# A feed-forward schedule that treats the last token of every 512 by itself

## The chip, the cores and the metric

One core of one Trainium2 chip runs the whole program. The metric is the device time of one execution in microseconds (us). Engines: PE (matmul), DVE (vector), ACT (scalar), POOL (GpSimd) and SP (which only issues DMAs here).

## The reference, cut to what matters

`x` holds 2048 tokens of 256 features, the context 1601. A cross-attention with four heads of 64 runs first, then a feed-forward with quantized weights and activations:

```python
x = x + xattn(ctx, layernorm(x), mask, ...)      # keys: 1601 of the context and the 2048 tokens
x = x + ffn(layernorm(x), w1, conv_w, conv_b, w2)

def ffn(x, w1, conv_w, conv_b, w2):
    h = bit_linear(x, w1)                        # 256 -> 1024, rows of x rounded to 8 bits each
    h = depthwise_conv1d(h, conv_w, conv_b)      # over the tokens, 3 taps: t-1, t, t+1
    return bit_linear(silu(h), w2)               # 1024 -> 256, rows rounded again
```

The convolution is all that couples neighbouring tokens in the feed-forward: a token needs the hidden values of the one before and the one behind it.

## The kernel before, in words

**Stages.** A prologue loads and normalizes the tokens and makes keys, values and queries. Then comes a loop of 80 beats. A unit is 512 queries of one pair of heads; there are 8 units (0 to 7), two for each 512 tokens, of ten beats each, and a beat takes three of the 29 blocks of 128 keys (the last beat of a unit two). In a beat PE makes the scores `st`, ACT their exponentials `pt`, and PE multiplies these with the values into `ot`. The sum of the exponentials is collected beside that: some `pt` are added into `acc` and `acd` by DMAs that POOL issues, the others into `vec` by DVE. In the second and third beat of the next unit DVE joins the sums, PE adds them up into `dn`, and DVE takes its reciprocal and divides (`finish_unit`, line 683).

After every second unit the 512 tokens that are complete go through `block_steps` (727) in four blocks of 128, one a beat from the sixth beat of the next unit on: output projection `po`, residual and statistics, normalization, rounding to 8 bits, and a transpose into `xq_all` (rounded features by token) with the factors of the tokens, repeated on all partitions, in `ib_all`.

**The feed-forward** works on eight groups of 256 tokens (0 to 7), each in four slots of 256 of the 1024 hidden values. A slot has `hidden` (809, four matmuls into `ph` for 258 tokens, one more at either end), `dequantize` (820, DVE: `h` = `ph` times `ib_all`), `taps` and `last_tap` (829, 846: the convolution into `pre` on ACT, DVE and POOL) and `silu` (856, ACT, into `t`; in the loop it needs another activation table than the exponential, and one is loaded before and behind it). After its slots a group has `magnitudes` (912: `m`, the largest value of each token, in two halves), `columns` and `scales` (920, 926: `m` transposed by PE into `tpa`, reduced by DVE to `am`, factors `qsc`, and on POOL `cm`), `scales_spread` (934: `cm` transposed into `tpb` and copied by ACT to `tb`), `rounding` (940: two halves of the hidden values, each a product into `t` and a rounding into `hq`), and `product` (950: for each 128 tokens eight matmuls `py`, then on DVE `res` = `py` times factor plus residual, and on SP the store).

**The order** is written out by hand. `plan` holds calls by beat (`at`, 594), and `feed_forward(g, k, slots)` (964) enters those of a group whose first slot is at beat k: `hidden` and `dequantize` at k-1, then a slot every second beat; `columns` and `scales` at k+11, `scales_spread` and the first `rounding` at k+13, the second at k+14, `product` at k+15. Group 1 ends at token 511, whose convolution needs token 512, which is complete some 20 beats later than token 511. Before, groups 0 to 3 begin at beats 30, 48, 56 and 68, and the first slot of group 4 at beat 76 (1000). Each engine carries out its instructions in the order of the program (`InOrder`, 162).

**Behind the loop** (from line 1060 on) two of the three taps of half a slot move to PE, as matmuls with diagonal matrices (`end_taps`, `end_convolve`, `end_last_tap`, `end_silu`). The last 512 tokens go through the block steps (`head`, 1100), and beside them `tick(i)` (1119) takes one slot after another, 15 slots in all: three of group 4 and those of groups 5, 6 and 7. What `plan` still holds (the end of group 3) is called one call per tick (`rest`, 1115). Each `product` makes its `res` at once. `compare` of the last unit follows at tick 15, and the flag `behind` is made at the very end; by it the program decides whether a second, slower version of the layer has to run (it does not here).

**PSUM.** In the loop three double banks (`big`, 153) hold `st`, `ph` and `py` in turn, one bank holds `ot`, and a single bank (`bank`, 156, one buffer) serves `dn`, `tpm`, `tpa`, `tpb`, `po` and `tpy` in turn.

Of the kernel before, what the change touches and what calls it, by code (L numbers as in the profile page):

```python
# [10 lines left out]
F32 = mybir.dt.float32  # L11
# [8 lines left out]
P = 128  # L20
# [9 lines left out]
def layer(  # L30
# [86 lines left out]
    OFF = 1  # L117
    xq_all = const.tile([P, ND, NL + 2 * OFF], BF16, name="xq_all")
    units1 = const.tile([P, NQB], F32, name="units1")
    for edge in (OFF - 1, OFF + NL):  # L120
        nc.gpsimd.memset(xq_all[:, :, edge : edge + 1], 0.0)

    q_un = [const.tile([P, NPAIR * QW], F32, name=f"q_un{g}") for g in range(NU)]
# [29 lines left out]
    def big(name):  # L153
        return ps_b.tile([P, 2, 512], F32, tag="big", name=name)
# [442 lines left out]

    def quant_scales(amax, n, vector=nc.vector):

        vector.tensor_scalar(amax, amax, QUANT_EPS, None, ALU.max)  # L600
        sc = sm.tile([P, QPG], F32, tag="qsc", name="qsc")
        vector.reciprocal(sc[:, :n], amax)
        vector.tensor_scalar(sc[:, :n], sc[:, :n], 127.0, None, ALU.mult)
        return sc

    def product_units(amax, i):

        vector.tensor_scalar(amax, amax, w_mean[:, i : i + 1], 1.0 / 127.0, ALU.mult, ALU.mult)

    def as_rows(cols, n):  # L610

        cm = sm.tile([P, QPG, P], F32, tag="cm", name="cm", bufs=3)
        for i in range(n):
            gpsimd.tensor_scalar(cm[:, i, :], ones, cols[:, i : i + 1], None, ALU.mult)
        return cm

    def repeat_rows(tp, cm):

        for i in range(QPG):
            tensor.transpose(tp[:, i, :], cm[:, i, :], ident)  # L620
# [6 lines left out]
    with att:  # L627
# [166 lines left out]

        fp = att.enter_context(tc.tile_pool(name="fp", bufs=1 if behind is None else 2))
        ib_all = fp.tile([P, NL + 2], F32, name="ib_all", bufs=1)
        for edge in (0, NL + 1):
            nc.gpsimd.memset(ib_all[:, edge : edge + 1], 0.0)

        NP = NH // 2  # L800
# [1 line left out]
        groups_ = [{} for _ in range(NG)]  # L802
        chunk = {}
        where = {
            "ph": big, "py": lambda: big("py")[:, 0, :D],
            "t": lambda: fp.tile([P, G, NC2], F32, tag="t", name="t", bufs=3),
        }

# [11 lines left out]
        def dequantize(s):  # L820
            t0 = s // NP * G
            h = fp.tile([P, 2, G + 2], F32, tag="h", name="h", bufs=2)
            vector.tensor_tensor(
                h, chunk[s]["ph"][:, :, : G + 2],
                ib_all[:, t0 : t0 + G + 2].unsqueeze(1).to_broadcast([P, 2, G + 2]), ALU.mult,
            )
            chunk[s]["h"] = h
# [74 lines left out]
        def end_silu(s, j):  # L902
            g, c = s // NP, s % NP * 2
            if c % NC2 == 0 and j == 0:
                groups_[g].setdefault("t", []).append(where["t"]())
            t = groups_[g]["t"][c // NC2][:, :, c % NC2 + j]
            if j == 0:
                scalar.activation(t, chunk[s]["ph"][:, 0, :G], AF.Silu, bias=cb_sb[:, c : c + 1])
            else:
                scalar.activation(t, chunk.pop(s)["pre"][:, 1, :], AF.Silu)  # L910
# [12 lines left out]
            for i in range(QPG):  # L923
                tensor.transpose(b["tp"][:, i, :], b["m"][:, ts(i, P)], ident)

        def scales(g):
            b = groups_[g]
            b["unit"] = sm.tile([P, QPG], F32, tag="am2", name="am2")
            vector.tensor_reduce(b["unit"], b.pop("tp"), AX.X, ALU.max)
            sc = quant_scales(b["unit"], QPG, vector)  # L930
            b["cm"] = as_rows(sc, QPG)
            product_units(b["unit"], 1)

        def scales_spread(g):
            tb = bank("tpb", [P, QPG, P])
            repeat_rows(tb, groups_[g].pop("cm"))
            groups_[g]["tb"] = fp.tile([P, G], F32, tag="tb", name="tb")
            scalar.copy(groups_[g]["tb"], tb.rearrange("p i t -> p (i t)"))

        def rounding(g, i):  # L940
            b = groups_[g]
            t = b["t"][i]
            vector.tensor_tensor(
                t, t, b["tb"].unsqueeze(2).to_broadcast([P, G, NC2]), ALU.mult
            )
            if i == 0:
                b["hq"] = fp.tile([P, G, NH], BF16, tag="hq", name="hq", bufs=1)
            vector.tensor_scalar(b["hq"][:, :, ts(i, NC2)], t, MAGIC, -MAGIC, ALU.add, ALU.add)

        def product(g, i):  # L950
            b = groups_[g]
            py = where["py"]()
            for c in range(NH):
                tensor.matmul(
                    py, b["hq"][:, ts(i, P), c], w2T[:, c, :], start=(c == 0), stop=(c == NH - 1)
                )
            qb = g * QPG + i
            res = fp.tile([P, D], F32, tag="res", name="res")
            vector.scalar_tensor_tensor(
                res, py, b["unit"][:, i : i + 1], x1[qb], ALU.mult, ALU.add  # L960
            )
            nc.sync.dma_start(out_t[:, qb, :], res)

        def feed_forward(g, k, slots, pace=2):

            for n in range(slots):
                s, t = g * NP + n, k + n * pace
                for m, call in (
                    (-1, hidden), (-1, dequantize), (0, taps), (1, last_tap), (3, silu),
                ):  # L970
                    at(t + m, lambda call=call, s=s: call(s), LATE)
                if n % 2:
                    at(t + 4, lambda n=n: magnitudes(g, n // 2), LATE)
            if slots < NP:
                return
            t = k + NP * pace
            for m, call in (
                (3, columns), (3, scales), (5, scales_spread), (5, lambda g: rounding(g, 0)),
                (6, lambda g: rounding(g, 1)), (7, lambda g: product(g, 0)),
                (7, lambda g: product(g, 1)),  # L980
            ):
                at(t + m, lambda call=call: call(g), LATE)

# [12 lines left out]
        for j in beats[0]:  # L996
            pts[0, j] = exponential(0, j, early.pop(0) if early else scores(0, j))

        for g, k in enumerate((30, 48, 56, 68)):
            feed_forward(g, k, NP)  # L1000
        feed_forward(4, 76, 1)
        at(NB * len(units) - 6, lambda: diagonals(0), LATE)
        at(NB * len(units) - 2, lambda: diagonals(1), LATE)

# [60 lines left out]
        def y_bank(name):  # L1065
            return ps_y.tile([P, QW], F32, tag="y", name=name)

        where.update(
            ph=lambda name: ps_h.tile([P, 2, 512], F32, tag="ph", name=name),
            py=lambda: y_bank("py")[:, :D],  # L1070
            t=lambda: ptp.tile([P, 2, QW], F32, tag="pt", name="t").rearrange(
                "p h q -> p (h q)"
            ).rearrange("p (t c) -> p t c", c=NC2),
# [38 lines left out]
                if i < NSUB:  # L1112
                    run(i, RESIDUAL, INVERSE)

        rest = [call for key in sorted(plan) for call in plan.pop(key)]
        slots = list(range(4 * NP + 1, NG * NP))
        N = len(slots)

        def tick(i):
            if 0 <= i - 2 < N:  # L1120
                end_silu(slots[i - 2], 1)
            if 0 <= i - 1 < N:
                end_silu(slots[i - 1], 0)
            if i < N:
                dequantize(slots[i])
            if 0 <= i - 1 < N:
                end_last_tap(slots[i - 1])
            if i < N:
                end_taps(slots[i])
            for g in range(4, NG):  # L1130
                n = i - ((g - 4) * NP - 1)
                if n == 4:
                    magnitudes(g, 0)
                if n == 6:
                    magnitudes(g, 1)
                    columns(g)
                    scales(g)
                if n == 7:
                    scales_spread(g)
                if n == 8:  # L1140
                    rounding(g, 0)
                    rounding(g, 1)
            if i + 1 < N:
                hidden(slots[i + 1])
            if i < N:
                end_convolve(slots[i])
            if 1 <= i <= NSUB:
                run(i - 1, TURN)
            for g in range(4, NG):
                if i == (g - 4) * NP + 7:  # L1150
                    product(g, 0)
                    product(g, 1)

        for sub in range(NSUB):
            run(sub, BIAS)
        hidden(slots[0])
        for i in range(N + 6):
            head(i)
            tick(i)
            if i >= 2 and rest:  # L1160
                rest.pop(0)()
            if i == N:
                compare(len(units) - 1, r)
        assert not rest

    if behind is not None:
        worst = sm.tile([P, 1], F32, tag="worst", name="worst")
        nc.vector.tensor_reduce(worst, near, AX.X, ALU.min)
        nc.vector.tensor_scalar(worst, worst, 0.5, None, ALU.is_lt)
        many = bank("many", [P, 1])  # L1170
        nc.tensor.matmul(many, ones, worst, start=True, stop=True)
        nc.vector.tensor_copy(behind, many)


@with_exitstack
# [41 lines left out]
```

## Time and profile before

| | before |
|---|---|
| median of 3 runs | 695.08 us (694.35 to 696.06) |
| the profiled execution | 695.91 us, span of its instructions 693.9 us |
| mean granted PE clock | 0.973 |
| busy: PE, DVE, ACT, POOL | 630.2, 465.6, 423.5, 277.3 us |
| loop, first to last `ot` matmul | 113.0 to 590.9 us |
| behind the loop | 590.9 to 693.9 us |
| activation table loads | 34, 1283 ns each |

The page cuts the span in 40 slices of 17.3 us and gives each engine's busy share in tenths. All matmul and vector calls are recorded at one line of a helper (L170), so instructions are told apart by their tiles: `py<-w2T,hq` is the matmul that writes `py` from `w2T` and `hq`. A row of the timeline has start, length, engine, operation, tiles and shapes, and in brackets the idle time of the engine before it and what ended that.

### The profile page before, as it was taken

To read this page: it belongs to the slowest core of one execution; us is meant where nothing else is said; L and a number is where in the kernel's file an instruction comes from. 1 tells how busy PE (TensorE), PEld (TensorE's weight loads), DVE (VectorE), ACT (ScalarE), POOL (GpSimd) and SP (SyncE) were. 2 spreads that over 40 slices of the span, in tenths; PEclk is the share of its full clock that TensorE was granted. 3 is DMA by queue.
4 is the path that set the end of the run, shared out by engine and by line. 5 is a ranking of instruction groups with operands and counts; after the bars stand their busy time and mean duration, and the time that the engine had idled before them with its cause. 6 is when DMAs were issued, how large, how long until landed. Compare 5 with 4: busy or idle time off the path is not lost. (4 is left out here: it accounts for less than half of the span.)

```text
span 693.9 us, 8026 instructions
## 1 busy us (share of the span) xinstructions
PE 630.2 (91%) x2796; PEld 266.8 (38%) x2796; DVE 465.6 (67%) x790; ACT 423.5 (61%) x534; POOL 277.3 (40%) x333
## 2 busy tenths in 40 slices
PE   4999898999999999999999999998899999766753
PEld 2555563333333333333334333333333433445532
DVE  3658774332822865696387779667976889895884
ACT  2556556555555544679845478997576799254440
POOL 2656663211221335244154444434344466432220
PEclk9999999999999999999999999999999999988985
DMA  7600003684876765478658447865474555000000
GB/s 238 169 0 1 0 1 102 128 161 96 182 144 160 151 122 106 113 132 166 152 128 161 92 106 140 167 133 141 93 147 91 142 100 109 0 0 17 15 31 20
DMA packets 32220, 72.12 MB, mean 104 GB/s; under 512 B 7531, under 2 KB 16940, under 8 KB 32172
## 3 DMA queue, kind: packets, MB, share of 16 engines
q0 software_dynamic: 16560, 60.30, 42.9%
q1 hardware_dynamic: 14524, 10.45, 5.1%
q10 hardware_dynamic: 1088, 0.79, 0.3%
q8 instruction: 24, 0.39, 0.2%
q14 instruction: 24, 0.20, 0.1%
HBM read 9.13 MB, written 2.10 MB: 16 GB/s over the span
## 5 line engine op out<-in xcount | busy, mean ns | idle before, releaser
L170 ACT ACTIVATE pt<-st,bias 128x1024 f32<-128x1024 f32 x232 | 242.9, 1113 | 123.9 <-issue 63.0
L170 PE MATMUL st<-q_un,kT 64*128 64x512 f32 x928 | 222.2, 607 | 5.0 <-DVE res L170 1.8
L170 PE MATMUL ot<-pt,v_sb 128*64 128x512 f32 x928 | 216.6, 600 | 0.1
L170 DVE TENSOR_TENSOR vec<-vec,pt 128x1024 f32<-128x1024 f32 x107 | 137.5, 1285 | 40.3 <-ACT pt L170 36.3
L170 PEld LDWEIGHTS st<-q_un,kT 64*128 64x128 f32 x928 | 82.7, 186 | 124.6 <-issue 89.3
L170 PEld LDWEIGHTS ot<-pt,v_sb 128*64 128x64 f32 x928 | 60.2, 136 | 136.9 <-issue 130.4
L170 POOL DMA_DIRECT2D acd<-pt x54 | 44.9, 832 | 127.2 <-ACT pt L170 60.7
L170 POOL DMA_DIRECT2D acc<-pt x61 | 52.7, 864 | 69.6 <-ACT pt L170 51.2
L170 POOL TENSOR_TENSOR pre<-pre,side 128x512 f32<-128x512 f32 (+1 forms) x32 | 38.4, 1201 | 57.0 <-DVE pre L170 51.8
L170 PE MATMUL kv<-wkv_sb,feat 128*128 128x512 f32 (+1 forms) x116 | 53.6, 605 | 0.0
L170 ACT ACT_TABLE_LOAD x34 | 43.6, 1283 | 16.2 <-DMA lb<-in_L_xattn_ln_l_b_dram 7.5
L170 POOL TENSOR_TENSOR ss<-ss,neg_half 128x8 f32<-128x8 f32 (+1 forms) x23 | 39.2, 1702 | 1.9
L170 POOL TENSOR_SCALAR cm<-ones,units 128x128 f32<-128x128 f32 x16 | 11.8, 739 | 60.1 <-DVE units L170 57.7
L170 DVE TENSOR_TENSOR h<-ph,ib_all 128x516 f32<-128x516 f32 x32 | 22.0, 687 | 20.1 <-PE ph L170 18.5
L170 DVE TENSOR_REDUCE ss<-sq 128x8 f32<-128x512 f32 (+1 forms) x23 | 15.5, 672 | 29.7 <-ACT sq L170 29.5
L170 DVE COPY oT<-ot 128x512 f32<-128x512 f32 x8 | 5.5, 692 | 44.0 <-PE ot L170 43.9
L170 PE MATMUL ph<-h,dg 128*128 128x256 f32 x90 | 25.9, 430 | 7.3 <-DVE h L170 7.3
L170 ACT ACTIVATE t<-pre 128x512 f32<-128x512 f32 (+1 forms) x32 | 29.7, 929 | 2.3 <-POOL pre L170 2.0
L170 DVE RECIPROCAL r<-dn 128x512 f32<-128x512 f32 (+1 forms) x11 | 27.3, 2480 | 5.6 <-PE dn L170 5.6
L170 PEld LDWEIGHTS kv<-wkv_sb,feat 128*128 128x128 f32 (+1 forms) x116 | 21.4, 193 | 22.4 <-issue 21.5
L170 ACT ACTIVATE side<-h,cw_sb 128x256 f32<-128x256 f32 x66 | 29.7, 507 | 0.0
L170 PE MATMUL py<-w2T,hq 128*128 128x256 bf16 x128 | 20.5, 318 | 8.3 <-DVE hq L170 8.3
(128 smaller groups left out, 712.2 us busy)
## 6 DMA issues: line engine op xcount, KB each, us to landing
acc<-pt POOLq DMA_DIRECT2D x61, 512.0 KB, 5.1
acd<-pt POOLq DMA_DIRECT2D x54, 512.0 KB, 4.7
tok<-in_x_dram SPq DMA_DIRECT2D x4, 512.0 KB, 6.0
w_sb<-in_L_ffn_w_dram SPq DMA_DIRECT2D x4, 512.0 KB, 5.9
q_un<-in_x_dram SPq DMA_DIRECT2D x4, 512.0 KB, 3.8
out_dram<-res SPq DMA_DIRECT2D x16, 128.0 KB, 1.7
tok<-in_ctx_dram SPq DMA_DIRECT2D x3, 512.0 KB, 4.7
wkv_sb<-in_L_xattn_W_kv_dram ACTq DMA_DIRECT2D x1, 512.0 KB, 7.4
```

Source lines behind the costliest of these rows:

```text
L170: return tc.keep_in_program_order(getattr(self.engine, name)(*args, **kwargs))
```

## The change

The hidden values of tokens 511, 1023 and 1535 are made apart, once all tokens are there. In the columns of `xq_all` and `ib_all` a zero stands in place of the first token of the next 512 for the groups that run earlier; what they give for the last token of each 512 is not stored (127 rows of 128). Three edge tokens then pass in ticks 4 to 11 through small copies of all steps.

So group 1 can begin at beat 38, and the groups begin at 30, 38, 50, 58 and 70 and the first slot of group 5 at 78: five groups and a slot lie in the loop instead of four and a slot. Behind it there are 11 slots and one empty place (between groups 5 and 6) instead of 15 slots, and three more ticks instead of six. There, a group's `res` comes in the tick after its `py`, behind the next `columns`. The order within a tick is new: the last taps stand between `columns` and `scales`. The last group makes `cm` on ACT, rounds straight from PSUM, by 128 tokens instead of by half the hidden values, and each `py` follows its half; `compare` and the flag stand ahead of that. The factor 1/127 is put into the first step of `quant_scales`, which drops one small DVE instruction per call.

```diff
-    for edge in (OFF - 1, OFF + NL):
+    for edge in (OFF - 1, *range(OFF + QW, OFF + NL + 1, QW)):
         nc.gpsimd.memset(xq_all[:, :, edge : edge + 1], 0.0)
...
-        vector.tensor_scalar(amax, amax, QUANT_EPS, None, ALU.max)
+        vector.tensor_scalar(amax, amax, QUANT_EPS, 1.0 / 127.0, ALU.max, ALU.mult)
         sc = sm.tile([P, QPG], F32, tag="qsc", name="qsc")
         vector.reciprocal(sc[:, :n], amax)
-        vector.tensor_scalar(sc[:, :n], sc[:, :n], 127.0, None, ALU.mult)
...
+            if by_scalar:
+                scalar.activation(cm[:, i, :], ones, AF.Copy, scale=cols[:, i : i + 1])
+            else:
+                gpsimd.tensor_scalar(cm[:, i, :], ones, cols[:, i : i + 1], None, ALU.mult)
...
+            if last:
+                groups_[g]["tb"] = tb.rearrange("p i t -> p (i t)")
+                return
...
+            rows = P - 1 if qb % NSUB == NSUB - 1 and qb < NQB - 1 else P
+            nc.sync.dma_start(out_t[:rows, qb, :], res[:rows, :])
...
+        def edge_residuals():
...
+            for e in range(NE):
+                nc.sync.dma_start(edge["x"][e : e + 1, :], x1[e * NSUB + NSUB - 1][P - 1 : P, :])
+        def edge_hidden():
...
+            for c in range(NH):
+                for k in range(ND):
+                    tensor.matmul(
+                        edge["ph"][:, c], w1T[:, k, ts(c, P)], edges(xq_all[:, k, :], OFF),
+                        start=(k == 0), stop=(k == ND - 1),
+                    )
+        def edge_convolve():
...
+            for e in range(NE):
+                t0 = 1 + e * QW + QW - 2
+                vector.tensor_tensor(
+                    h[:, :, e, :], edge["ph"][:, :, e, :],
+                    ib_all[:, t0 : t0 + 3].unsqueeze(1).to_broadcast([P, NH, 3]), ALU.mult,
+                )
+            for e in range(NE):
+                vector.tensor_tensor(h[:, :, e, :], h[:, :, e, :], cw_sb, ALU.mult)
+            edge["pre"] = edge_space(P, [NH, NE])
+            vector.tensor_reduce(edge["pre"], h, AX.X, ALU.add)
...
+        outputs = []
+        def end_product(g, i):
+            product(g, i)
+            outputs.append((g, i))
+            if not where["later"]:
+                output(*outputs.pop())
...
-        for g, k in enumerate((30, 48, 56, 68)):
+        for g, k in enumerate((30, 38, 50, 58, 70)):
             feed_forward(g, k, NP)
-        feed_forward(4, 76, 1)
+        feed_forward(5, 78, 1)
...
-        slots = list(range(4 * NP + 1, NG * NP))
+        slots = [*range(5 * NP + 1, 6 * NP), None, *range(6 * NP, NG * NP)]
+        for n, call in enumerate((
+            edge_hidden, edge_convolve, edge_silu, edge_magnitudes, edge_scales, edge_rounding,
+            edge_product, edge_output,
+        )):
+            at(NB * len(units) + 4 + n, call, LATE)
...
+            if 6 in at_:
+                magnitudes(at_[6], 1)
+                columns(at_[6])
+            while outputs:
+                output(*outputs.pop(0))
+            if slot(i) is not None and slot(i - 1) is not None:
+                end_last_tap(slot(i - 1))
+            if slot(i) is not None:
+                end_taps(slot(i))
+            if 6 in at_:
+                scales(at_[6], at_[6] == NG - 1)
+                if at_[6] == NG - 1:
+                    flag()
...
+            if 7 in at_ and at_[7] == NG - 1:
+                g = at_[7]
+                scales_spread(g, True)
+                for n in range(QPG):
+                    for half in range(2):
+                        rounding(g, half, ts(n, P))
+                    product(g, n)
+                for n in range(QPG):
+                    output(g, n)
```

## The prediction

> **What bounds the kernel now.** The page's slices come first: PE is 80 to 90% busy or more, until the last six.
>
> ```profile
> span 693.9 us, 8026 instructions
> ...
> PE   4999898999999999999999999998899999766753
> ...
> DVE  3658774332822865696387779667976889895884
> ...
> PEclk9999999999999999999999999999999999988985
> ```
>
> Then the table by stretches, cut where DVE's copy of `ot` ends one unit of ten beats and the next begins: units 1 to 7, then the end up to its tick 4, and the rest.
>
> ```profile
> core 0: us, PE busy (x) PEld busy (x) DVE busy (x) ACT busy (x) POOL busy (x), PEclk, DMA share, GB/s
> 164.76:220.03 55.27, 55.27 (x243) 18.61 (x243) 26.83 (x27) 30.35 (x29) 12.18 (x15) 1.00 0.72 149
> 220.03:280.22 60.19, 60.19 (x266) 21.75 (x265) 38.47 (x63) 31.43 (x33) 20.71 (x29) 1.00 0.64 130
> 280.22:339.40 59.18, 58.45 (x265) 20.18 (x265) 39.77 (x52) 47.62 (x55) 22.02 (x25) 1.00 0.69 143
> 339.40:403.29 63.89, 63.42 (x289) 24.20 (x289) 46.26 (x79) 35.98 (x40) 26.84 (x31) 1.00 0.58 120
> 403.29:462.54 59.25, 58.84 (x269) 20.50 (x269) 45.22 (x58) 52.53 (x62) 23.30 (x26) 1.00 0.74 152
> 462.54:532.53 69.99, 65.47 (x300) 25.11 (x300) 54.34 (x94) 49.73 (x55) 32.06 (x40) 1.00 0.52 107
> 532.53:590.89 58.36, 56.91 (x265) 20.52 (x266) 51.17 (x61) 49.50 (x57) 33.86 (x33) 1.00 0.56 120
> 590.89:620.85 29.96, 20.33 (x88) 12.82 (x88) 25.13 (x69) 11.12 (x24) 11.80 (x21) 0.89 0.00 0
> 620.85:693.90 73.05, 41.65 (x207) 29.64 (x205) 50.48 (x89) 25.62 (x51) 17.87 (x21) 0.79 0.06 20
> ```
>
> Subtract PE's busy time from each length. Units 1 to 5 lose 0 to 0.7 us: the loop is bound by PE. Unit 6 loses 4.5 and unit 7 1.5, where feed-forward brings DVE to 54.34 and 51.17 us. The end, 103.0 us, is a DVE chain (75.6 us busy) with 27 us of holes. The largest, in the timeline of DVE:
>
> ```profile
> 632.76 0.48 DVE L170 SCALAR_TENSOR_TENSOR res<-py,am,q_un 128x256 f32<-128x256 f32 x1 [3.96 <-PE py L170]
> ...
> 636.37 0.48 DVE L170 SCALAR_TENSOR_TENSOR res<-py,am,q_un 128x256 f32<-128x256 f32 x1 [2.14 <-PE py L170]
> ```
>
> and behind the last `silu` (done at 669.7):
>
> ```profile
> 674.24 0.48 DVE L170 SCALAR_TENSOR_TENSOR res<-py,am,q_un 128x256 f32<-128x256 f32 x1 [1.22 <-PE py L170]
> ...
> 682.29 1.23 DVE L170 TENSOR_TENSOR t<-t,tb 128x1024 f32<-128x1024 f32 x1 [2.19 <-ACT tb L170]
> ...
> 688.98 0.48 DVE L170 SCALAR_TENSOR_TENSOR res<-py,am,q_un 128x256 f32<-128x256 f32 x1 [1.22 <-PE py L170]
> ```
>
> **The end, part by part.** (1) One whole group leaves it. In the steady part the first `h` of one group starts at 644.01 and that of the next at 659.21: −15.2 us. (2) Group 4's last half comes in place of group 3's, one step earlier: `m` (1.21 + 0.42) and `am` with its small ones (0.42 + 2 x 0.17 + 0.22), +2.6. (3) `res` is put a tick later, behind the next `h` and `m`. The holes of 3.96 and 2.14 go, but after group 5's rounding only an `h` (0.69) lies ahead of `res`, and PE needs some 1.5 us there (in its timeline 12 `py` took 1.53 there), so 1 us of wait is left: −5. (4) Last group. `m` no longer stands behind `res` (hole 1.22) and `compare` (0.42 + 0.69 + 0.69); `compare` moves into the 2.19 hole. Rounding by halves lets PE start on eight of the last 16 `py` earlier; the two `res` come after both, so one wait of 1.2 goes. Four more DVE starts and `many`'s return to DVE take about 1 back. −4. (5) Some seven dropped `qsc` steps on the path at 0.17: −1.2. (6) The edge tokens add 16 small DVE instructions (0.15 to 0.48, as `am` and `res`; 3.4 together) and five hand-overs to PE, ACT and POOL, each with a tick to spare. No row shows them in this place. If all are covered the price is 3.4; if each costs the shortest wait for PE in the fences it is 3.4 + 5 x 1.2 = 9.4; less than nothing is excluded, since all of it is new DVE work. I take 4.5, near the lower row, as one or two ticks will be short. Their three loads and the three one-row stores go through SP, which sends x's last reload ahead of the end's stores and otherwise only outputs; nobody waits for it before the last `res`. The six more zeroed columns are POOL's, before the loop; there POOL waits for DVE, and without that cover they would cost six short instructions, under 1 us.
>
> Sum −15.2 + 2.6 − 5 − 4 − 1.2 + 4.5 = −18.3. Bounds: −13 (edge waits in full) and −22 (no `res` wait left, edges 3.4, no second price in (4)).
>
> **The loop, part by part.** Groups 1 to 4 start at beats 38, 50, 58, 70 (48, 56, 68 and 76 before). Relative to the block steps at 44 and 64, every pair of groups now stands as groups 1 and 2 stand before, two beats later. PE gains one group, by the groups of 100 to 590 us: 68 `ph` matmuls take 10.3 us in 17 slots, four slots 2.4; 48 `py` take 5.9 in three groups, one 2.0; `tpa` and `tpb` 0.44 each. +5.3 us, all on PE's path. It is the floor.
>
> DVE gains some 15 us: `h` 4 x 0.69, `pre` 8 x 0.46 and 4 x 0.80, `t` 2 x 1.38, `hq` 2 x 0.70, `res` 2 x 0.48, and the first `m`, 1.21; twelve dropped `qsc` steps give 2.0 back. By the beats, 7 fall in unit 4: before, group 1 had an `h` at 47, the `pre` at 48 and an `h` and last tap at 49 there (2.7); now it has two `h` (41, 43), three pairs of `pre` (40 to 44), three last taps, both `m` (44, 48) and its `am` (49). That makes 53.3 us of 46.3, unit 6's level of today. 2.7 fall in unit 3 (beats 37 to 39), 2.2 in unit 5, little in 6 and 7. In units 5 and 7 the second rounding (beats 52 and 72) now falls on the beat of the 3.35 us reciprocal; before, that was so in unit 6 alone, whose holes on PE lie at 479 to 496 us, around that beat. Three prices for the waits: unit 7 has 88% DVE and loses 1.5, unit 6 78% and loses 4.5, unit 5 76% and loses 0.4. For unit 4 I take +2.5, between 0 and 4; for 5 and 7 +1 each (0 to 4); for 6 −0.5 to +2: +4.2 in all, 0 to 14.
>
> POOL's adds also cost DVE: `vec<-vec,acd` took 2.00 us at 479.29, beside POOL's `pre` at 478.94 (1.27), against 1.22 alone; one group has four such pairs of adds, up to 4 x 0.8, within the bounds above. ACT gains 4 x (3 x 0.51 + 1.15 + 2 table loads of 1.28) = 21 us; unit 4's 36 becomes 57 of some 68: covered.
>
> Here a rule speaks against the change: the Trainium skill, page ScalarE: Activation LUTs, section What ACT_TABLE_LOAD costs, puts a drain of about 1.38 us behind each load, 2.66 in all. By it the group would cost ACT an estimated 32 us, unit 4 would be full and PE would wait for the exponentials. The trace has a load from 476.40 to 477.68 and its `silu` at 477.70, so I go by 1.28 alone.
>
> The loop: +5.3 + 4.2 = **+9.5**, bounds +5.3 and +19.
>
> **Sum.** −18.3 + 9.5 = −8.8 us. The profiled execution took 695.91 us around its span of 693.9, 0.8 above the median 695.08 of three; the change of −8.8 is put on the median: 686.3, rounded to **686**.
>
> **Rivals.** *A: loop at PE's floor*, end at its best: +5.3 − 21 = −15.7, 679. For it: unit 7's 1.5 at 88% DVE. Against: unit 6. *B: DVE pays it back*: units 4, 5 and 7 each lose 4 more as unit 6 does, and the edge hand-overs all wait: +5.3 + 12 − 14 = +3.3 at worst, −2 in the middle, 693. For it: DVE would be near 80% in four units on end. *C: slower, by the single PSUM bank.* `dn`, `tpm`, `tpa`, `tpb`, `po` and `tpy` share one buffer, and PE, in order, stops at the next of them until DVE or ACT has read the one before. Groups 0 to 3 end with `tpa` and `tpb` among them, eight hand-overs. At the 3.35 us reciprocal each: 27 + 5.3 − 18.3 = +14, 709. It decides from (18.3 − 5.3) / 8 = 1.6 us each. Against: in 400 to 590 us PE's waits at these tiles sum to 2.3 us (`dn` 1.1, `tpa` and `tpb` 0.6 each). That the groups don't move is no rival: the order on DVE has group 1's `h` in beat 37.
>
> **Chances.** Forecast 0.60, A 0.18, B 0.14, C 0.08. Below 693.0 lie the forecast nearly whole, A, and half of B: faster 0.83. From 693.0 to 697.2 (0.3%, what a measurement here can tell from no change) 0.08, slower 0.09. The range takes the forecast's bounds, half of A and most of B: 678.5 to 695.
>
> **What would show it.** Loop's last `ot` at 600 instead of 590.9 (A 596; B 605 and more; C over 609, with PE waiting at bank tiles). Unit 4 some 68 to 69 us, with PE idle for 2 to 4. The end 103.0 to 85 us, no `res` wait above 1.5, less than 3 us from last `am` to first `t`. Wrong if edge steps carry DVE holes of a microsecond each, or if unit 5 or 7 loses what unit 6 does.

## The result, and the profile after

The changed kernel takes **703.3 us** (median of five runs, 702.99 to 705.29) against 694.35 (692.79 to 696.06) of the kernel before beside it: a ratio of 1.0135, 95% interval 1.0113 to 1.0157. It is slower by 9 us where 8.8 us of gain were forecast. The profiled execution took 703.27 us, its span is 701.4. The profiled execution of before took 695.91, 1.6 above the median beside the changed kernel, so the two profiles show 7.5 us where the medians show 9.0.

The page's slices of the kernel after:

```profile
span 701.4 us, 8050 instructions
...
PE   4999998999999999999988998999899989864854
...
DVE  3668774334732864785598858666988596868976
...
PEclk9999999999999999999999999999999999995985
```

Between slices 21 and 33 PE's digit falls to 8 five times; before it did so in slices 28 and 29 alone. The table by stretches says how much. The cuts are the same as before (units 1 to 7, the end up to its tick 4, the rest):

```profile
core 0: us, PE busy (x) PEld busy (x) DVE busy (x) ACT busy (x) POOL busy (x), PEclk, DMA share, GB/s
...
279.28:338.83 59.55, 59.01 (x269) 20.50 (x269) 40.69 (x54) 48.77 (x58) 22.22 (x25) 1.00 0.69 143
338.83:409.72 70.89, 66.40 (x297) 25.44 (x298) 58.35 (x88) 53.06 (x58) 33.96 (x39) 0.98 0.54 110
409.72:477.09 67.37, 62.38 (x288) 22.50 (x289) 45.73 (x64) 48.61 (x59) 23.36 (x27) 1.00 0.63 131
477.09:546.34 69.25, 64.78 (x296) 24.73 (x297) 57.28 (x88) 53.74 (x59) 34.87 (x39) 1.00 0.57 117
546.34:610.51 64.17, 60.30 (x271) 21.13 (x270) 50.31 (x64) 45.95 (x56) 29.06 (x31) 0.97 0.48 104
610.51:646.80 36.29, 20.15 (x80) 12.45 (x79) 26.73 (x66) 11.72 (x23) 15.88 (x25) 0.78 0.00 0
646.80:701.40 54.60, 32.97 (x179) 24.30 (x179) 41.05 (x86) 19.49 (x39) 12.17 (x14) 0.78 0.07 22
```

Against the table of before, unit by unit: unit 3 +0.4, unit 4 **+7.0**, unit 5 **+8.1**, unit 6 −0.7, unit 7 **+5.8**; together +20.5 us. PE's busy time grows by 9.8 of these and its idle time by 10.8. The end of the kernel, 103.0 us before, takes 90.9: −12.1, of which its beginning (to tick 4) costs 6.3 more and the rest 18.4 less. With −0.9 ahead of unit 3, which starts that much earlier in this execution, they make the 7.5 us between the two spans. The forecast had +9.5 for the loop and −18.3 for the end: 11 us of the miss lie in the loop and 6 in the end.

Where unit 4 loses is seen in the timeline of PE (in brackets the idle time ahead of a row and what ended it):

```profile
366.78 0.41 PE L171 MATMUL tpb<-ident,cm 128*128 128x128 f32 x2 [1.58 <-DVE nm L171]
...
371.65 2.08 PE L171 MATMUL st<-q_un,kT 64*128 64x512 f32 x4 [2.10 <-DVE h L171]
373.66 1.78 PE L171 MATMUL po<-wo_sb,oT 128*128 128x256 f32 x4
```

and in that of DVE at the same time:

```profile
363.06 2.24 DVE L171 TENSOR_SCALAR pre<-h,cw_sb,cb_sb 128x256 f32<-128x256 f32 x1
365.22 1.21 DVE L171 TENSOR_TENSOR vec<-vec,pt 128x1024 f32<-128x1024 f32 x1
366.36 0.28 DVE L171 TENSOR_REDUCE nm<-tpm 128x1 f32<-128x128 f32 x1
...
366.87 0.42 DVE L171 TENSOR_SCALAR within<-r 128x512 bf16<-128x512 f32 x1
367.33 0.69 DVE L171 SCALAR_TENSOR_TENSOR within<-r,within 128x512 bf16<-128x512 f32 x1
368.05 0.69 DVE L171 TENSOR_REDUCE near<-within 128x1 f32<-128x512 bf16 x1
368.66 1.22 DVE L171 TENSOR_TENSOR t<-t,tb 128x1024 f32<-128x1024 f32 x1
369.91 0.69 DVE L171 TENSOR_SCALAR hq<-t 128x1024 bf16<-128x1024 f32 x1
370.51 0.48 DVE L171 SCALAR_TENSOR_TENSOR pre<-h,cw_sb,pre 128x256 f32<-128x256 f32 x1
370.91 0.69 DVE L171 TENSOR_TENSOR h<-ph,ib_all 128x516 f32<-128x516 f32 x1
```

DVE has no gap here. It carries group 1's taps (`pre`), the unit's own maximum and `compare` (`nm`, `within`, `near`) and group 0's rounding (`t`, `hq`) one behind the other, and only then the next `h` of group 1. PE waits twice: at `tpb`, which shares the single bank with the `tpm` that `nm` reads, and at `st`, which takes the double bank whose `ph` that `h` reads. The beat (the 44th, counted by its `ot`) takes 12.97 us against 6.93 before. Unit 6, which had such a beat before already (the 64th, 10.53 us), has it again (11.34). The two rows behind the hole of 2.10 are slow too: the same four `po` take 1.13 us in unit 6.

The six largest summed waits of PE from 330 us to the loop's end (in a row: the sum in us, how often, the longest):

```profile
PE st L171 <- DVE h L171: 5.5, 4, 2.1
PE tpb L171 <- DVE nm L171: 3.1, 2, 1.6
PE dn L171 <- DVE vec L171: 2.9, 2, 1.5
PE st L171 <- ACT pt L171: 2.0, 6, 0.4
PE tpm L171 <- DVE r L171: 1.5, 2, 0.7
PE tpa L171 <- ACT ib_all L171: 1.3, 2, 0.6
```

Four of these six rows, 13.0 of 16.3 us, end with DVE; the exponentials, ACT's `pt`, end only 2.0. In unit 5 it is DVE that waits first, in its own timeline:

```profile
425.49 1.23 DVE L171 TENSOR_TENSOR t<-t,tb 128x1024 f32<-128x1024 f32 x1 [2.43 <-ACT tb L171]
426.75 0.69 DVE L171 TENSOR_SCALAR hq<-t 128x1024 bf16<-128x1024 f32 x1
...
428.36 2.00 DVE L171 TENSOR_TENSOR vec<-vec,acd 128x1024 f32<-128x1024 f32 x1
430.28 2.47 DVE L171 TENSOR_TENSOR vec<-vec,pt 128x1024 f32<-128x1024 f32 x2
```

Group 1's rounding stands in DVE's order ahead of the unit's sums, and waits 2.43 us for `tb`. `dn`, which needs the first of these sums (`acd`, done at 430.36), starts on PE at 430.41, after a wait of 1.47 us; on DVE the two other sums and the reciprocal (from 432.66) follow. So PE waits in a unit where DVE has 45.73 us of work in 67.37, 68%. In all the unit is 8.1 us longer, 4.6 of them idle time of PE; its other waits, 0.3 to 1.0 us each in sum, are for `pt`, `res`, `h` and `tpa`.

The largest holes in DVE's timeline in the end:

```profile
615.00 0.96 DVE L171 RECIPROCAL r<-dn 128x128 f32<-128x128 f32 x1 [2.55 <-PE dn L171]
...
629.87 0.42 DVE L171 TENSOR_REDUCE am<-tpa 128x2 f32<-128x256 f32 x1 [2.62 <-PE tpa L171]
...
642.92 1.23 DVE L171 TENSOR_TENSOR t<-t,tb 128x1024 f32<-128x1024 f32 x1 [2.16 <-ACT tb L171]
...
669.14 0.18 DVE L171 TENSOR_TENSOR edge<-edge,edge_tb 128x24 f32<-128x24 f32 x1 [1.41 <-PE edge_tb L171]
...
677.49 1.22 DVE L171 TENSOR_TENSOR t<-t,tb 128x1024 f32<-128x1024 f32 x1 [2.93 <-ACT tb L171]
```

The waits of `res` for `py`, 3.96 and 2.14 before, are gone (none above 0.61). In their place DVE waits for `tb` and `tpa`.

### The profile page after: what moved, and what is told of

Same layout as the page of the kernel before. It is cut to its first block, busy times and chain, and to the rows that moved or that the text cites. A ratio compares the mean times of both kernels' runs of the same rounds, so it can differ in the third digit from the quotient of the medians.

```text
span 701.4 us, 8050 instructions
## 1 busy us (share of the span) xinstructions
PE 630.1 (90%) x2798; PEld 264.7 (38%) x2798; DVE 472.7 (67%) x794; ACT 432.6 (62%) x542; POOL 281.3 (40%) x342
## 4 chain that ended last, share of the span: by engine, by line
PE 70%; DVE 18%; ACT 5%; DMA 3%; issue 2%; POOL 1%; SPq 0%; DVEq 0%; ACTq 0%; POOLq 0%
PE ot L171 24%; PE st L171 24%; PE kv L171 6%; DVE vec L171 3%; PE ph L171 3%; DMA acc<-pt 2%; PE py L171 2%; PE qp L171 2%; PE po L171 2%; DVE r L171 2%; DVE t L171 2%; DVE pre L171 2%; ACT pt L171 2%; PE tp L171 1%; DVE h L171 1%
## 5 line engine op out<-in xcount | busy, mean ns | idle before, releaser
L171 PE MATMUL st<-q_un,kT 64*128 64x512 f32 x928 | 224.5, 612 | 9.4 <-DVE h L171 5.5
L171 DVE TENSOR_TENSOR vec<-vec,pt 128x1024 f32<-128x1024 f32 x107 | 143.0, 1336 | 40.4 <-ACT pt L171 36.5
L171 POOL DMA_DIRECT2D acc<-pt x61 | 53.3, 874 | 72.6 <-ACT pt L171 48.4
L171 POOL TENSOR_TENSOR pre<-pre,side 128x512 f32<-128x512 f32 (+1 forms) x32 | 41.6, 1299 | 86.4 <-DVE pre L171 83.4
L171 ACT ACTIVATE t<-pre 128x512 f32<-128x512 f32 (+1 forms) x32 | 31.6, 987 | 10.8 <-POOL pre L171 10.6
L171 DVE TENSOR_TENSOR h<-ph,ib_all 128x516 f32<-128x516 f32 x32 | 21.9, 685 | 21.4 <-PE ph L171 21.4
L171 DVE TENSOR_REDUCE ss<-sq 128x8 f32<-128x512 f32 (+1 forms) x23 | 15.5, 673 | 28.7 <-ACT sq L171 28.6
L171 ACT ACTIVATE side<-h,cw_sb 128x256 f32<-128x256 f32 x74 | 32.8, 506 | 0.0
L171 PE MATMUL ph<-h,dg 128*128 128x256 f32 x66 | 21.6, 477 | 10.5 <-DVE h L171 10.5
L171 ACT ACTIVATE sq<-kv 128x512 f32<-128x512 f32 (+1 forms) x15 | 8.7, 583 | 29.5 <-PE kv L171 29.4
```

Of the source, the lines that this page charges most:

```text
L171: return tc.keep_in_program_order(getattr(self.engine, name)(*args, **kwargs))
```

## The experiments

All diffs are against the changed kernel. Loop and end are from the profiled executions (before: end of the loop 590.9, the end 103.0; after: 610.5 and 90.9); ratios are against the kernel before in the same job. Two limits hold for differences of the end. The profiled execution of before is 2.4 to 2.8 us above the medians of 693.1 to 693.5 beside these runs, and no trace shows in which part. And the same end takes 91.4 to 93.7 us in the five runs below that keep the starts and edit only the loop, where the changed kernel's takes 90.9; so 2 to 3 us of the end are not settled by one pair of profiles.

**The new end with the old starts.** The groups start as before, and the edge steps, which that makes needless, are left out.

```diff
-        for g, k in enumerate((30, 38, 50, 58, 70)):
+        for g, k in enumerate((30, 48, 56, 68)):
...
-        feed_forward(5, 78, 1)
+        feed_forward(4, 76, 1)
...
-        slots = [*range(5 * NP + 1, 6 * NP), None, *range(6 * NP, NG * NP)]
+        slots = [*range(4 * NP + 1, NG * NP)]
...
-            at_ = {i + 1: 5, i - 4: 6, i - 7: 7}
+            at_ = {i + 1: 4, i - 3: 5, i - 7: 6, i - 10: 7}
```

> Groups begin at beats 30, 48, 56, 68 and 76 as before, no edge tokens; only the new order behind the loop is kept. If the gain behind the loop comes from that order (later res, the last group's order, fewer qsc steps) as my steps 3 to 5 have it, the loop ends at about 590 us as before and the end takes some 92 to 94 us instead of 103: 683 to 686 us. If the new order is worth nothing and only the group that left the end made it shorter, it is 693 to 696.

Measured: 689.91 us, ratio 0.9944 (0.9921 to 0.9967). Loop 591.5, end 96.8. By the two profiles the new order of the end is worth 6.2 us (by the medians of the job, 693.11 and 689.91, it is 3.2), not the 10.2 of steps (3) to (5). DVE's timeline shows where the rest stayed:

```profile
608.46 1.22 DVE L171 TENSOR_TENSOR t<-t,tb 128x1024 f32<-128x1024 f32 x1 [3.03 <-ACT tb L171]
...
633.99 1.23 DVE L171 TENSOR_TENSOR t<-t,tb 128x1024 f32<-128x1024 f32 x1 [1.38 <-ACT tb L171]
...
650.06 1.23 DVE L171 TENSOR_TENSOR t<-t,tb 128x1024 f32<-128x1024 f32 x1 [2.79 <-ACT tb L171]
...
664.64 1.22 DVE L171 TENSOR_TENSOR t<-t,tb 128x1024 f32<-128x1024 f32 x1 [1.29 <-ACT tb L171]
```

With `res` out of the way the first rounding comes up before `tb` is there: 8.5 us of waits for `tb`. With the old starts the time is a gain, with the new ones a loss: what turns it lies with the starts.

**Groups at an even distance of ten beats.**

```diff
-        for g, k in enumerate((30, 38, 50, 58, 70)):
+        for g, k in enumerate((30, 40, 50, 60, 70)):
```

> Groups begin at 30, 40, 50, 60, 70: groups 1 and 3 two beats later, so that their roundings leave the beats before and on the reciprocal; the work is the same. If the place of a group's end within the unit makes PE wait (place), units 5 and 7 lose their waits for vec and res and fall by 3 to 4 us each, 4 and 6 by 1: 693 to 697 us. If DVE's amount of work alone does it (load), the time stays within 2 us of the changed kernel: 701 to 705.

Measured: 711.52 us, ratio 1.0273 (1.0241 to 1.0306). Units 4 to 7 take 71.3, 68.0, 71.3 and 66.7 us, beats 44, 54, 64 and 74 take 12.95, 9.62, 12.99 and 11.94. That is more than either reading had allowed. The theory that the rounding on the beat of the reciprocal is at fault falls: with another place for it the long beats come again, in every unit.

**No `compare` in units 0 to 6.** It leaves out the test that sets the flag for these units (`near` is set to 1.0), which is 1.8 us of DVE per unit, in the beat of unit 4's stop and of unit 6's.

```diff
+        nc.gpsimd.memset(near, 1.0)
...
-                at(k + 3, lambda: compare(u, box["r"]), END)
```

> Leaves out the check of the reciprocals (compare) of units 0 to 6, three DVE instructions of 1.8 us in each unit's fourth beat; that part of the flag is missing. If PE's holes come from DVE being behind (load), h is read 1.8 us earlier in units 4 and 6, the hole of 2.1 us and the half clock behind it go, and units 4 and 6 fall by 3 to 4 us each, 5 and 7 by 1 to 2: 693 to 696 us. If the single bank of PSUM makes the holes, only little of this goes: 700 to 702.

Measured: 697.98 us, ratio 1.0069 (1.0038 to 1.0100). Units 4 to 7 take 68.3, 66.1, 68.2 and 62.5 us, and the hole ahead of `st` falls from 2.10 to 1.09. The four units are 6.7 us shorter for 7.2 us of DVE work taken out, though DVE is only 68 to 83% busy in them by the table. Half of the 6.7 is idle time of PE (3.3 us); the other half is PE's busy time, as the granted clock is 1.00 in units 4 and 7 here, for 0.98 and 0.97. So DVE's work ahead of an `h` is paid by PE; the time lies between the two readings, and the share alone does not tell it.

**`tpa` and `tpb` in the double banks** instead of the single one, in the loop.

```diff
-            b["tp"] = bank("tpa", [P, QPG, P])
+            b["tp"] = where["tp"]("tpa")
...
-            tb = bank("tpb", [P, QPG, P])
+            tb = where["tp"]("tpb")
...
+            "tp": lambda name: big(name)[:, 0, :G].rearrange("p (i t) -> p i t", t=P),
```

> In the loop tpa and tpb take a buffer of the three double banks instead of the single bank. If the hand-overs of the single bank make the holes (bank), PE's waits at tpm, tpa and tpb (5.9 us) and at dn go, and the half clock with them: 693 to 697 us. If DVE is behind (load), PE only stops later, at the next buffer that DVE has to read: 701 to 705, or more, as the double banks are shorter by one for a while.

Measured: 707.53 us, ratio 1.0216 (1.0187 to 1.0245), slower than the changed kernel. PE's waits from 330 us on:

```profile
PE st L171 <- DVE h L171: 7.4, 2, 3.7
PE dn L171 <- DVE vec L171: 2.9, 2, 1.5
```

The wait of `tpb` is gone, and the hole ahead of `st` has grown from 2.1 to 3.7 us, by just as much. DVE's `h` comes at the same time as before the edit (370.97 for 370.91). So the tiles `tpa` and `tpb` in the single bank (rival C) are not the cause of this stop: they are one of several places in which PE meets the same late DVE. The run has two limits: a double bank is missing for a while, and `dn`, `tpm`, `po` and `tpy` stay in the single bank.

**No edge steps.** It leaves out the three edge tokens, which are then not stored.

```diff
-        )):
+        )[:0]):
...
-        edge_residuals()
```

> Leaves out the edge steps: the last tokens of the first three 512s are not made. Predicted price of the steps 4.5 us, bounds 3.4 and 9.4. The changed kernel's trace has about 3 us of DVE work for them and one hole of 1.4 us at edge_tb: 698 to 700 us, loop unchanged. If their hand-overs also push the ticks around them (tb waits of 2.2 and 2.9 us go), 694 to 697.

Measured: 699.90 us, ratio 1.0096 (1.0057 to 1.0135). The loop is unchanged, the end takes 87.8 instead of 90.9: 3.05 us for the edge steps (3.4 by the medians). Two waits of the changed kernel belong to them: the 1.41 for `edge_tb`, and 1.6 of the 2.93 for `tb`, which is 1.29 without them. In return their work covers others: without it a `res` waits 1.07 and an `h` 0.66 where they stood.

**Less in a burst.** The starts are moved so that no group begins while the one before it ends.

```diff
-        for g, k in enumerate((30, 38, 50, 58, 70)):
+        for g, k in enumerate((35, 43, 55, 63, 70)):
```

> Groups begin at 35, 43, 55, 63, 70: roundings at beats 48 to 49, 56 to 57, 68 to 69, 76 to 77, none in the second to fifth beat of a unit, where DVE has the joins, the reciprocal and compare. The work is the same. If that burst of DVE makes the holes (burst), units 4 to 7 come to some 66, 62, 66 and 61 us instead of 70.9, 67.4, 69.3 and 64.2: 685 to 690 us. If DVE's total in the loop is what counts, wherever it falls (load), 701 to 706, and moving may cost as in the run with starts ten beats apart.

Measured: 707.92 us, ratio 1.0210 (1.0166 to 1.0254). Beat 44 takes 6.56 us again, and units 3 to 7 are 5 us shorter together (326.2 against 331.2). But new long beats come (49, 51, 59, 69: 8.9 to 9.4 us each), and PE's largest waits are now for ACT:

```profile
PE st L171 <- ACT pt L171: 4.7, 7, 1.8
PE tpb L171 <- ACT ib_all L171: 3.5, 2, 1.7
PE ph L171 <- ACT pt L171: 2.7, 2, 1.7
PE py L171 <- DVE h L171: 1.9, 1, 1.9
```

and the end takes 99.6 us; DVE waits 6.73 us for `tb` in the loop's last beats and 3.92 for the next `dn`, but whether these waits make it longer was not tested. The theory is right in part: the burst of beat 44 can be moved away, but with these starts the time of the whole is above even the second reading.

**Group 4's `columns` a tick earlier**, in the end's beginning.

```diff
-                (3, columns), (3, scales), (5, scales_spread), (5, lambda g: rounding(g, 0)),
+                (3 - (g == 4), columns), (3, scales), (5, scales_spread), (5, lambda g: rounding(g, 0)),
```

> Group 4's columns are called at tick 0 instead of tick 1, so that tpa is ahead of the first block's tpy in the single bank. If the wait of DVE's am for it (2.62 us) is what makes the end's start longer, it goes and the start of the end falls by 2 to 3 us: 700 to 701 us. If it only moves to the next hand-over of the bank: 702.5 to 704.

Measured: 701.80 us, ratio 1.0122 (1.0070 to 1.0174). The hole of 2.62 ahead of `am` is gone and the end takes 87.8 us, 3.06 less; the loop, in which nothing is changed, ended 1.3 later in this execution (611.8), and the time as a whole cannot be told from the changed kernel's (1.5 us less by the medians, two runs). In the changed kernel `tpa` stood behind the first block's `tpy`, which holds the same single bank: for this wait it is the bank.

**The last two together**, starts 35, 43, 55, 63, 70 and the earlier `columns`.

> Both edits, starts 35, 43, 55, 63, 70 and group 4's columns at tick 0. If burst and bank in the end's start are both right: 682 to 688 us, faster than the kernel before. If neither: 701 to 706.

Measured: 703.19 us, ratio 1.0162 (1.0106 to 1.0218). Loop 606.0, as with these starts alone, end 94.3, 5.3 shorter than with them alone. The time is that of the second reading: the earlier `columns` help the end, and neither edit cures the loop.

**Old starts, roundings a tick later.** The first experiment's kernel, in which both roundings of a group now come in one tick, the later of the two, and group 3's first a step later.

```diff
-                (3, columns), (3, scales), (5, scales_spread), (5, lambda g: rounding(g, 0)),
+                (3, columns), (3, scales), (5, scales_spread), (5 + (g == 3), lambda g: rounding(g, 0)),
...
-                rounding(at_[7], 0)
             if 8 in at_ and at_[8] != NG - 1:
+                rounding(at_[8], 0)
                 rounding(at_[8], 1)
```

> The starts of before and the new order behind the loop, but with both roundings of a group in the tick after scales_spread, as before, and group 3's first rounding a beat later. In the run with the old starts DVE waits 3.0, 1.4, 2.8 and 1.3 us for tb, once a group: the waits that took the place of the res waits. If that is where the expected 4 us of the new order went, most of these 8.5 us go: 682 to 687 us. If the chain over POOL, PE and ACT is what takes the time, whatever DVE does meanwhile, 688 to 691.

Measured: **685.61 us** (682.89 to 686.63), ratio 0.9872 (0.9844 to 0.9901): faster than both kernels. Loop 590.5, end 92.5. The waits for `tb` ahead of a rounding are gone, and the largest hole of DVE behind the first `dn` (1.97) is 1.31. With that place for the rounding, the new order of the end is worth 10.5 us by the profiles and 7.9 by the medians of the job (693.54 and 685.61); the prediction had 10.2 for it. Of the 8.5 us of waits some 4.3 come back, by both measures.

**No table loads.** It puts a copy in place of `silu`, so ACT keeps its table throughout the loop; the function itself is left out.

```diff
-            scalar.activation(t.rearrange("p t c -> p c t"), chunk.pop(s)["pre"], AF.Silu)
+            scalar.activation(t.rearrange("p t c -> p c t"), chunk.pop(s)["pre"], AF.Copy)
```

> In the loop the silu of groups 0 to 4 is left out (a copy with the same shape stands in its place), so ACT loads no tables there: some 40 us less of ACT. If ACT's longer work in the loop makes PE wait (act), units 4 to 7 lose most of their holes: 690 to 695 us. If DVE is behind (load), PE's waits at h, vec, res and the bank stay and only the 2 us at pt go: 699 to 702.

Measured: 697.12 us, ratio 1.0046 (1.0025 to 1.0068). Units 4 to 7 take 67.6, 66.8, 67.6 and 62.6 us; loop 603.7. In the changed kernel the page counts 40 loads, 51 us of ACT; taking out those that `silu` needs gives back some 7 us in the loop, 4.3 of them PE's busy time: the granted clock is 1.00 in all four units. PE still stops at `tpb` for `nm` (3.1) and at `dn` for `vec` (2.9). But the largest row, `st` for `h`, falls from 5.5 us to 1.3. In beat 44 PE has

```profile
370.29 1.13 PE L171 MATMUL st<-q_un,kT 64*128 64x512 f32 x4 [0.41 <-ACT pt L171]
```

and DVE has, no earlier than with the loads,

```profile
371.25 0.69 DVE L171 TENSOR_TENSOR h<-ph,ib_all 128x516 f32<-128x516 f32 x1
```

So this `st` starts ahead of the `h` for which it waits 2.10 us in the changed kernel, as soon as a `pt` is done. A late `h` thus costs PE nothing at an `st` that does not need the double bank which the `h` reads. Why it is not needed here, and whether the table loads or this is what gives the 7 us, the run does not show. Neither reading had it so: the stops at `tpb` and `dn` stayed, the one at `h` did not.

**Group 1 without its end.** `columns`, `scales`, `rounding` and `product` of group 1 are left out, its slots stay.

```diff
-            if slots < NP:
+            if slots < NP or g == 1:
```

> Leaves out the end of group 1 (columns to product; its 256 tokens are not stored), its slots stay. Its share of PE is 2.9 us, of DVE some 6. If a group's end is the dear part, unit 5 falls from 67.4 to 59 to 61 us, 694 to 697 in all. If it is the slots beside another group's end, unit 5 falls by the 3 us of PE only and unit 4 stays at 70.9: 699 to 701.

Measured: 697.49 us, ratio 1.0051 (1.0029 to 1.0074). Unit 4 is unchanged (70.9), unit 5 falls from 67.4 to 59.5: −7.8 us, of which 3.4 are PE's busy time and 4.4 its idle time.

**No group 1 in the loop.** The whole group is left out.

```diff
-        for g, k in enumerate((30, 38, 50, 58, 70)):
+        for g, k in ((0, 30), (2, 50), (3, 58), (4, 70)):
```

> Leaves out group 1 altogether in the loop, the other starts as in the changed kernel. If the price of the fifth group is its 5.3 us of PE, 698 us. If it is that and holes in units 4 and 5, as the two traces say, unit 4 comes to 64 to 65 us, unit 5 to 60 to 61 and the whole to 687 to 691.

Measured: 688.77 us, ratio 0.9923 (0.9901 to 0.9945). Units 3 to 7 take 59.0, 62.8, 59.5, 70.9 and 63.5 us. PE's timeline around beat 44, with no row that waits:

```profile
366.66 2.80 PE L171 MATMUL ot<-pt,v_sb 128*64 128x512 f32 x12
369.39 2.85 PE L171 MATMUL st<-q_un,kT 64*128 64x512 f32 x12
372.17 1.13 PE L171 MATMUL po<-wo_sb,oT 128*128 128x256 f32 x4
```

This divides the loop's +20.5: with the same number of groups as before, only later by two beats, units 3 to 7 take 315.7 us, 5.0 more than before, nearly all of it in unit 7 (63.5 for 58.4). Group 1 itself adds 15.5 us for some 5.3 us of PE work: 0.6 in unit 3, 8.1 in unit 4, where its slots stand beside group 0's end, 7.8 in unit 5, where its end stands beside group 2's slots, and about −1 in units 6 and 7 together.

## Why the prediction was wrong

**The end: −12.1 instead of −18.3; the direction was right.** Three runs divide it, each part into the beginning (to the `h` behind the last block's steps, tick 4) and the rest: the new order with the old starts gives +3.5 and −9.7; the group that leaves, from there to the run without edge steps, +3.7 and −12.7; the edge steps −0.8 and +3.9. These sum to the +6.3 and −18.4 of the table. (1) One whole group less was set at −15.2, four places of 3.8 us; but with the empty place between groups 5 and 6 the places fall from 15 to 12, and three of 3.8 are 11.4 (an estimate; no run leaves the empty place out). The −12.7 lies near that. (2) Group 4's last half cost 3.7 us, not 2.6: I counted DVE's instructions, and left out that its `tpa` goes behind a `tpy` in the one bank; the earlier `columns` gave 3.06 back. (3) to (5) gave 6.2, not 10.2: the `res` waits went as forecast, but I named no wait that is late next. It was the rounding's for `tb`, 8.5 us with the old starts; a tick later for the rounding gives 10.5, or 7.9 by the medians. (6) The edge steps cost 3.05 us, or 3.4 by the medians, not 4.5; a part of them is covered by waits, which my lower bound of 3.4 did not allow for. The edge term and the 3.06 are hardly larger than the spread of the end. Two sums were loose as well: the bound of −22 adds up to −21.4, and DVE's list to 14.0 us, not 15 (15.6 were measured in units 3 to 7).

**The loop: +20.5 instead of +9.5. This step failed,** in the term "+4.2 in all, 0 to 14" for the waits; it made the forecast's gain a loss. The floor of 5.3 us of PE work is near the truth: busy time grew by 9.8, of which the half clock (see the last section) makes some 3.3, by (1 − 0.98) x 70.9 + (1 − 0.97) x 64.2; 1.2 are left that no run assigns. Against the 4.2 stand 10.8 us of idle time and these 3.3, together 14.1, the end of the range that I gave. Three things were wrong.

- *Unit 4* was given +2.5 above its PE work, with 4 as ceiling after unit 6's 4.5; it lost 4.0 in idle time (0.5 to 4.5) and 1.4 to the clock. DVE's work there was forecast at 53.3 us and is 58.4: DVE's instructions are longer beside POOL's (see the last section), which I had priced as "within the bounds above" and put into no sum.
- *Units 5 and 7* were given +1 each; their idle time grew by 4.6 and 2.4, and unit 7 lost 1.9 to the clock. I had seen that the second rounding falls on the beat of the reciprocal there, but priced the wait by DVE's share of busy time, and that does not tell it: the two have the lower share now (68 and 78%, for 82 and 83 in units 4 and 6). The trace of unit 5 shows that a wait for a hand-over, the 2.43 us for `tb`, passes through an engine that is 68% busy: the unit's own sums stand behind it in DVE's order, and `dn` on PE waits 1.47 us for them. Without group 1's end the unit has 0.6 us of idle time for 5.0. In unit 7 the cause is the move by two beats (it takes 63.5 us for 58.4 without group 1 too, 4.8 of them idle).
- *The ceiling* was taken from unit 6 as if a unit could have one such collision. The forecast's last test, "if unit 5 or 7 loses what unit 6 does", names what came in unit 5 (5.0 us idle, for unit 6's 4.5).

**The rivals.** A (PE's floor) is out. B named DVE as the payer, with 12 us of waits in units 4, 5 and 7; that is the nearest, with 10.8 us of idle time, and its end of −14 was near the −12.1. What it lacked were the 3.3 us of the clock; it had stopped at +3.3. C had the right direction (709 against 703): the loop ended behind 609 with PE waiting at bank tiles, 8.8 of the 16.3 us in the six rows, as its test wanted. But with `tpa` and `tpb` in other banks the wait only went on to the next buffer. So the place at which PE stops does not name the cause. DVE's own order is the best supported one: the trace of beat 44 has no gap in it, and 1.8 us less ahead of the `h` made the hole 1.0 shorter. It is not the whole, as the run without table loads shows: there the same late `h` held up no `st`.

**The rule that spoke against the change.** The Trainium skill, page ScalarE: Activation LUTs, section What ACT_TABLE_LOAD costs, would have added a drain behind each load. The traces show none: in beat 44 of the changed kernel two loads of 1.28 us start at 367.62 and 370.07, right behind rows that end at 367.60 and 370.05, and the ACTIVATE behind each starts at 368.91 and 371.36. The run without the loads gave some 7 us; how much of that is ACT's time is open.

**What is settled, and what is open.** Settled: with none of the three sets of starts that were tried does the loop take a whole further group at the price of its PE work. With the starts of the change it costs 15.5 us there and saves 9.0 in the end (96.8 with the old starts, 87.8 without edge steps). Left are the two beats (+5.0), the edge steps (+3.05) and the order of the end (−6.2): +8.4 in all, the 20.5 − 12.1 of the result. The gain lies in the order of the end, and can be had alone (685.6). Open: why the holes turn up at ACT's `pt` with starts 35 and 43, and why the end grows to 99.6 us with them; the chain over POOL, ACT and the `pt` buffers was not resolved. Open too: why an `st` waits for an `h` in one run and not in the other. A fourth buffer for `t`, which would let the end of a group wait for its own place, was not tried.

## What to carry to other kernels

Price a group of work that is moved beside others by the hand-overs in its chain, each against what stands ahead of it in the order of every engine it passes, and not by the engines' shares of busy time: an engine at 68% can pass a wait on (2.43 us on DVE became 1.47 on PE). Where one wait is taken away, name the next one in the same queue and move that too: with the roundings a tick later the order of the end was worth 4.3 us more. Before an expensive move is made, take the work out as a whole (here 15.5 us for 5.3 us of matmuls): it shows in one run what the place can bear.

## What the runs showed of the hardware

**Behind a short hole PE's clock can be halved, and behind the same hole it can stay.** PE's holes of 2.10 us in units 4 and 6 of the changed kernel are alike to the instruction. The table by stretches behind them, and behind unit 7's hole of 1.47 us:

```profile
371.60:374.60 3.00, 2.95 (x6) 1.34 (x7) 2.97 (x2) 2.70 (x3) 3.00 (x4) 0.50 0.33 64
509.80:512.80 3.00, 2.91 (x12) 1.32 (x14) 2.96 (x3) 3.00 (x4) 3.00 (x4) 1.00 0.37 66
...
566.10:569.60 3.50, 3.42 (x8) 1.01 (x10) 3.46 (x4) 0.97 (x3) 0.62 (x1) 0.51 1.00 186
```

The granted clock was 0.50 for 3 us behind the first, 1.00 behind the second, and 0.51 behind the shorter third. Unit 5 has a hole of 1.47 us ahead of `dn` as well, and behind it the four `dn` took 1.08 us, where unit 7's took 1.98. So the length of a hole does not decide alone. In 3 us PE made six matmuls instead of twelve, so some 1.5 us went behind the first and, by 0.51 over 3.5 us, 1.7 behind the third. The Trainium skill, page TensorE: Matmul & The Clock Gate, section HAM oscillation — how this bites in real kernels, gives the abstract rule "no PE-idle gaps >~3.4µs"; here the clock was halved behind holes of 1.5 and 2.1 us. The same page, section What's actually happening, says that the window in which activity is watched is free-running, and with that two equal holes with different outcomes agree; no run here shows the window itself.

**DVE's instructions can last longer beside POOL's.** In the fence of unit 4's DVE rows, `pre<-h,cw_sb,cb_sb` took 2.24 us; the median of its kind from 330 us to the loop's end is 0.41. POOL's timeline has, over it,

```profile
363.39 1.06 POOL L171 TENSOR_TENSOR q_un<-q_un,bo_sb 128x256 f32<-128x256 f32 x1
364.08 1.05 POOL L171 TENSOR_TENSOR side<-side 128x256 f32<-128x256 f32 x1
```

ending at 365.13, where DVE's row ends at 365.30. Before, the longest of these rows was 1.44 us. In unit 4 ten rows of DVE last over 0.3 us more than the median of their kind in the whole run, together by some 7 us, and each of them runs beside a TENSOR_TENSOR of POOL; before, two did, by 1.4. That is the size of what the forecast of 53.3 us missed to 58.4. The Trainium skill, page SBUF — State Buffer, section SBUF: two separate sides, names a port that GpSimd and Vector share; these rows agree with that, but no run here took POOL's work away to prove it.
